# A graph network on one core: a one-column product after each group of four tiles, in the first and the fourth layer

## The chip, the cores and the metric

The kernel runs on one core of a Trainium2 chip. The metric is the device time of one execution in microseconds (us); lower is better. The engines are named as the profile names them: PE is TensorE (PEld its weight loads), DVE VectorE, ACT ScalarE, POOL GpSimd, SP SyncE. L535 is line 535 of the kernel before.

## The reference

There are 12500 nodes with 32 features and 400000 edges, sorted by their target node. Four layers follow each other; each takes h = relu(layernorm(x)) and adds its result to x. Cut to what matters:

```python
def layer0(h, edge_feat, eps, src, dst):          # 32 features on each edge
    m = relu(h[src] + edge_feat)
    return (1 + eps) * h + segment_sum(m, dst)

def layer1(h, src, dst, edge_vec, emb, norm, W1, W2): ...   # tensor product with spherical harmonics
def layer2(h, row, col):                          # degree of each node as a source
    deg = segment_sum(ones, row)
    n = rsqrt(1 + deg)
    return n * (segment_sum((n * h)[col], row) + n * h)

def layer3(h, src, dst, sh, scalars, fc_w1, fc_w2):
    hid = relu(scalars @ (fc_w1 / sqrt(8))) * sqrt(2)        # [E, 256]
    w = (hid @ (fc_w2 / sqrt(256))).reshape(E, 4, 8, 8)
    s1, v1 = h[src][:, :8], h[src][:, 8:].reshape(E, 8, 3)
    s2, v2 = sh[:, 0], sh[:, 1:4]
    out_s = A_S * (einsum('eu,euw->ew', s1 * s2, w[:, 0]) + einsum('eui,ei,euw->ew', v1, v2, w[:, 1]) / sqrt(3))
    out_v = A_V * (einsum('eu,euw,ei->ewi', s1, w[:, 2], v2) + einsum('eui,euw->ewi', v1 * s2, w[:, 3])) / sqrt(3)
    return segment_sum(concat(out_s, out_v), dst) / sqrt(E / N)
```

## The kernel before

The 400000 edges are 3125 tiles of 128 edges, one edge to a partition. Sixteen tiles (`CT`) make a chunk, four tiles (`G`) a group; there are 196 chunks. Edges of a chunk have neighbouring targets, so that their sums fall into a window of nodes. The loops are unrolled, and a scheduler fixes the order of the instructions on each engine from the program's order and its dependencies; pools of rotating buffers (`bufs`) decide how far one engine may run ahead of another.

**Layer 0** (`layer0`, L626 to L702, run by `edges`, L574). For each group POOL gathers the source rows of four tiles by one indirect DMA each (`gather`, L535). `main` adds the edge features on DVE (L663) and takes relu on ACT (L664). `tail` calls `collect` (L451): DVE makes a one-hot matrix of the targets' places in the window (`oh`, L457), and four f32 products on PE (L460) add the tiles into `ps_win`. At the end of the chunk ACT copies the window out (`wsum`, L463) and `put_late` stores it. The second half of `tail` counts how often each node is a source: DVE splits the index into `hi` and `lo` (L680 to L683), makes two bf16 one-hots `ohi` and `olo` (L687), and four bf16 products (L690) add them into the histogram `ps_deg`, which DVE adds to `deg` once a chunk (L693). The one-hots come from a pool with two buffers, `ps_win` and `ps_deg` have two buffers in PSUM each.

**Layers 1 and 2** run together (`edges12`, L760 to L1121). The change doesn't touch them.

**Layer 3** (`edges3`, L1252 to L1392). One chunk is worked on while the next one's weights are made and the one after that is gathered:

- `gather`: 16 indirect DMAs on POOL (L1274), one a tile, into one of four buffers `hs`, two chunks ahead.
- `hidden`: four times a chunk, two bf16 products (L1285) into `ps_h`, which has one buffer of two PSUM banks, and a relu on ACT into `hid` (L1287).
- `scalars`: four small operations on DVE (L1293 to L1299).
- `product(c, g)`: for each group, eight f32 products (L1310) of `hid` with the second weight make `ps_w` (two buffers of two banks). An f32 product shows as two PE records, so a group shows as 16. DVE multiplies `ps_w` with the gathered rows into `pa` (L1314), `ps` (L1316) and `pv` (L1318). `ps` is the last reader of the buffer `hs`.
- `outputs`: DVE reduces these (L1326 to L1334); `thirds` splits the result into three bf16 parts (ACT L472, DVE L474 and L476).
- `places`: ACT makes the one-hot matrix (L1340, L1341).
- `collect`: 16 bf16 products (L1346) into `ps_sum`, copied by ACT (L1349); `add`: one f32 product, the fold (L1352), and ACT's copy (L1354), which `put_late` stores.

Layer 3 uses seven PSUM banks: two for `ps_h`, four for `ps_w`, one for `ps_sum`. Its order of work for one chunk is written out by hand:

```python
for s in range(4):
    if now:
        product(now, s)
        places(now, 4 * s, 4 * s + 4)
    if c:
        ...   # s = 0: outputs, thirds; 1: thirds; 2: thirds, collect; 3: add
    if c + 1 < NW:
        hidden(cs[c + 1], s % 2, s // 2)
```

Of the kernel before, what the change touches and what calls it, by code (L numbers as in the profile page):

```python
# [8 lines left out]
F32 = mybir.dt.float32  # L9
# [5 lines left out]
PSUM = bass.MemoryType.PSUM  # L15

P = 128
D = 32
NP = 125
G = 4  # L20
# [17 lines left out]
def tiles_of(E):  # L38

    C = Q4 * B  # L40
    return E // C * (C // P) - (-(E % C) // P)
# [15 lines left out]
class GNN:  # L57
# [14 lines left out]
    def __init__(self, tc, ctx, a, out, E):  # L72
        self.tc, self.nc, self.ctx, self.a, self.out, self.E = tc, tc.nc, ctx, a, out, E
        self.N = a["x"].shape[0]
        self.J = self.N // NP
        self.T = a["src"].shape[1]
        self.CT = G * CG
        self.IT = self.CT * CPI0
        assert self.N % NP == 0 and self.T % self.IT == 0
        dram = ctx.enter_context(tc.tile_pool(name="dram", bufs=1, space=bass.MemoryType.DRAM))  # L80
        rows = self.N + P
        self.tabs = [
            [dram.tile([rows, D], F32, name=f"acc{l}_{k}", tag=f"acc{l}_{k}") for k in range(NTAB)]
            for l in range(4)
        ]
        self.feats = [dram.tile([rows, D], F32, name=f"feat{l}", tag=f"feat{l}") for l in range(4)]
        self.NW = self.T // self.CT
        self.real = tiles_of(E)


        self.emb8 = dram.tile([9, 8, self.NW, Q4 * B], BF16, name="emb8", tag="emb8")
        self.emb10 = dram.tile([9, 10, self.NW, Q4 * B], BF16, name="emb10", tag="emb10")
        self.mid = dram.tile([rows, D + 1], F32, name="mid", tag="mid")
        self.local = dram.tile([P, self.NW, self.CT + 1], F32, name="local", tag="local")
        self.n_e = dram.tile([P, self.T, 3], F32, name="n_e", tag="n_e")
        self.loc_t = dram.tile([self.NW, Q4 * B], F32, name="loc_t", tag="loc_t")
        self.n_t = dram.tile([4, self.NW, Q4 * B], F32, name="n_t", tag="n_t")
        self.dst_rows = dram.tile([P, self.T], I32, name="dst_rows", tag="dst_rows")
# [367 lines left out]
    def thirds(self, pool, c, step):  # L466
# [8 lines left out]
        else:  # L475
            nc.vector.tensor_tensor(c["f3"][:, :, 2, :], c["f"], c["f3"][:, :, 1, :], op=ALU.subtract)  # L476

    def get(self, pool, l, c):

        c["win"] = pool.tile([P, D], F32, name="win")  # L480
        self.nc.sync.dma_start(c["win"], self.feats[l][ds(self.first(c), P), :])
# [144 lines left out]
    def layer0(self):  # L626
        nc, tc, J = self.nc, self.tc, self.J
        if not self.fast:
            with tc.tile_pool(name="rest", bufs=1) as pool:
                for _ in self.rest(pool):  # L630
                    pass
        with ExitStack() as ctx:
            rest = None
            if self.fast:
                self.resident(ctx)
                rest = self.rest(ctx.enter_context(tc.tile_pool(name="rest", bufs=1)))
                for _ in range(TABS[0]):
                    next(rest)
            big = ctx.enter_context(tc.tile_pool(name="big0", bufs=LEAD + 4 if self.fast else 2))
            gp = ctx.enter_context(tc.tile_pool(name="gather0", bufs=AHEAD + 2))  # L640
            wp = ctx.enter_context(tc.tile_pool(name="work0", bufs=2))
            psum = ctx.enter_context(tc.tile_pool(name="psum0", bufs=2, space=PSUM))
            hist = ctx.enter_context(tc.tile_pool(name="hist0", bufs=2, space=PSUM))

            def load(col):
                if self.fast:
                    c = {"edge_attr_32": self.load(big, "edge_attr_32", col)}
                else:
                    c = {n: self.load(big, n, col) for n in ("src", "dst", "edge_attr_32")}
                    c["row"] = self.load_row(big, "dst_t", col)  # L650
                    c["rows"] = big.tile([P, self.CT], I32, name="rows")
                c["col"] = col
                return c

            def gather(c, t0):
                return self.gather(gp, "hs", 0, c["src"], t0, c)

            def front(c, t0, hs):
                return None

            def main(c, t0, hs, _):
                m = wp.tile([P, G, D], F32, name="m", bufs=3)
                nc.vector.tensor_add(m, hs, c["edge_attr_32"][:, t0 : t0 + G, :])  # L663
                nc.scalar.activation(m, m, AF.Relu)  # L664
                return m

            def tail(c, t0, m):
                if self.fast:
                    self.collect(0, wp, psum, c, m, t0)
                else:  # L670
                    eq = self.same(wp, c["dst"], c["row"], t0)
                    self.firsts(wp, eq, c["dst"], c["rows"], t0)
                    self.scatter(0, wp, psum, eq, m, c["rows"], t0)

                if t0 == 0:
                    c["deg"] = hist.tile([P, P], F32, name="ps_deg")
                hi = wp.tile([P, G], F32, name="hi")
                lo = wp.tile([P, G], F32, name="lo")
                s = c["src"][:, t0 : t0 + G]
                nc.vector.tensor_scalar(hi, s, -0.5 * (J - 1), 1.0 / J, op0=ALU.add, op1=ALU.mult)  # L680
                nc.vector.tensor_scalar_add(hi, hi, ROUND)
                nc.vector.tensor_scalar_add(hi, hi, -ROUND)
                nc.vector.scalar_tensor_tensor(lo, hi, -float(J), s, op0=ALU.mult, op1=ALU.add)  # L683
                ohi = wp.tile([P, G, NP], BF16, name="ohi")
                olo = wp.tile([P, G, J], BF16, name="olo")
                for oh, v, n in ((ohi, hi, NP), (olo, lo, J)):
                    nc.vector.tensor_tensor(oh, self.iota[:, None, :n].to_broadcast([P, G, n]),  # L687
                                            v[:, :, None].to_broadcast([P, G, n]), op=ALU.is_equal)
                for k in range(G):
                    nc.tensor.matmul(c["deg"][:NP, :J], lhsT=ohi[:, k, :], rhs=olo[:, k, :],  # L690
                                     start=t0 + k == 0, stop=t0 + k == self.CT - 1)
                if t0 + G == self.CT:
                    nc.vector.tensor_add(self.deg, self.deg, c["deg"][:NP, :J])  # L693
                    if not self.fast:
                        nc.scalar.dma_start(self.dst_rows[:, ds(c["col"], self.CT)], c["rows"])

            self.edges(load, gather, front, main, tail,
                       windowed=(lambda c, row: c.update(self.places_of(big, row), src=self.sources_of(c))) if self.fast else None, beside=rest)
        with tc.tile_pool(name="end0", bufs=1) as pool:
            agg = self.gather_sum(0, pool)  # L700
            nc.vector.tensor_add(self.x, self.x, agg)
            nc.vector.scalar_tensor_tensor(self.x, self.h, self.eps1, self.x, op0=ALU.mult, op1=ALU.add)  # L702
# [549 lines left out]
    def edges3(self):  # L1252

        nc, tc, CT = self.nc, self.tc, self.CT
        with ExitStack() as ctx:
# [3 lines left out]
            ph = ctx.enter_context(tc.tile_pool(name="ph3", bufs=1, space=PSUM))  # L1259
            pw = ctx.enter_context(tc.tile_pool(name="pw3", bufs=2, space=PSUM))  # L1260
            ps = ctx.enter_context(tc.tile_pool(name="ps3", bufs=1, space=PSUM))

            def fetch(c):
                row = c["no"]
# [25 lines left out]
            def scalars(c):  # L1290
# [7 lines left out]
                vv = c["vv"] = wp.tile([P, CT, 3, 8], F32, name="vv")  # L1298
                nc.vector.tensor_mul(vv.rearrange("p g i u -> p g (i u)"), hs[:, :, 8:32], sh[:, :, 0:1].to_broadcast([P, CT, 24]))  # L1299

            def product(c, g):

                if g == 0:
# [4 lines left out]
                for k in range(4):  # L1308
                    for m in range(2):
                        nc.tensor.matmul(w[:, k, :], lhsT=c["hid"][:, m, 4 * g + k].rearrange("p q s -> p (q s)"), rhs=self.w2b[:, m, :],  # L1310
                                         start=m == 0, stop=m == 1)
                gs = slice(4 * g, 4 * g + 4)
                hs = c["hs"][:, gs, :]
                nc.vector.tensor_mul(c["pa"][:, gs], w[:, :, 0:128].rearrange("p g (w u) -> p g w u", u=16),  # L1314
# [3 lines left out]
                nc.vector.tensor_mul(c["pv"][:, gs].rearrange("p g i (w u) -> p (g i) w u", u=8),  # L1318
                                     w[:, :, None, 192:256].to_broadcast([P, 4, 3, 64]),
                                     c["vv"][:, gs].rearrange("p g i u -> p (g i) u")[:, :, None, :].to_broadcast([P, 12, 8, 8]))  # L1320

            def outputs(c):
                sh = c["sh"]
# [225 lines left out]
```

## Time and profile before

| | |
|---|---|
| time, median of three runs | 20938.48 us (20915.86 to 20953.58) |
| the profiled execution | 20931.77 us, span 20930.0 us |
| busy: PE, DVE, POOL, ACT | 12599.4, 12740.1, 14745.9, 6408.9 us |
| layer 0, about 200 to 4700 us: PE, DVE, POOL busy in 300 to 4600 | 1709.25, 1919.45, 3127.78 of 4300 us |
| layers 1 and 2: the same in 5500 to 15400 | 6492.84, 6717.33, 7962.22 of 9900 us |
| layer 3: the same in 15500 to 20840 | 3833.59, 3470.09, 2948.99 of 5340 us |
| mean granted PE clock of the span | 0.84 |

The page has the busy time of each engine, then the span in 40 equal slices (each digit the busy share in tenths), then the chain of work that ended last, then the costliest groups. A group's line reads: line, engine, operation, output and input tile, count, then busy time and the mean ns of one, then the engine's idle time ahead of them and what ended it. The waits name the engine and line that waited, what it waited for, and the total, the number and the longest in us. A line of the timeline has the start, the length, the instruction and its count, and in brackets the idle time ahead of it. The ends of PE's products are modelled; "remote" is a wait whose releaser the trace doesn't show.

### The profile page before, as it was taken

How to read it: one execution, taken by the hardware profiler on the slowest of the kernel's cores; microseconds unless marked ns; L12 is line 12 of the kernel's file. 1: busy time of each engine (PE TensorE's matmuls, PEld its weight loads, DVE VectorE, ACT ScalarE, POOL GpSimd, SP SyncE). 2: the span in 40 equal slices, each digit the busy share in tenths (PEclk: the TensorE clock that was granted, in tenths of full speed). 3: DMA queues.
4: the chain of work that ended last, by engine and by line, in shares of the span. 5: the costliest groups of instructions: out<-in, count | busy, mean ns of one | idle time of the engine just before them, and what ended most of it. 6: DMA issues, size and time to landing. Idle time of an engine off the chain costs nothing.

```text
span 20930.0 us, 189759 instructions
## 1 busy us (share of the span) xinstructions
PE 12599.4 (60%) x56444; PEld 6767.2 (32%) x56444; DVE 12740.1 (61%) x25505; ACT 6408.9 (31%) x13844; POOL 14745.9 (70%) x12508
## 2 busy tenths in 40 slices
PE   2443433334766666666666666666637777777776
PEld 2333433331211111111111111111125555555554
DVE  3554444334766666666666666666746666666666
ACT  0001110002333333333333333333324444444444
POOL 5777777774788888888888888888755555555553
PEclk9999999998777777777777777777768888888888
DMA  2113332112444444444444444444411111111111
GB/s 96 46 45 111 113 91 74 23 23 72 98 89 90 88 91 90 89 89 90 90 90 90 90 90 90 90 90 90 92 39 23 23 23 23 23 23 23 23 23 30
DMA packets 1482594, 1406.96 MB, mean 67 GB/s; under 512 B 1055751, under 2 KB 1250897, under 8 KB 1426409
## 3 DMA queue, kind: packets, MB, share of 16 engines
q1 hardware_dynamic: 668550, 1143.45, 17.2%
q0 software_dynamic: 750000, 205.60, 12.0%
q10 hardware_dynamic: 62992, 45.63, 0.7%
q8 instruction: 448, 7.34, 0.1%
q14 instruction: 604, 4.94, 0.1%
HBM read 1156.82 MB, written 236.20 MB: 67 GB/s over the span
## 4 chain that ended last, share of the span: by engine, by line
DVE 27%; issue 20%; PE 15%; POOL 14%; another core or an unknown queue 13%; ACT 7%; DMA 4%; DVEq 0%; ACTq 0%; SPq 0%; POOLq 0%
DVE z L853 6%; POOL acc L1008 5%; POOL hs L809 5%; PE ps_w L1310 5%; POOL hs L535 4%; PE ps_y L850 4%; DVE pv L1318 1%; DMA hs<-feat,src_all 1%; PE ps_o L860 1%; ACT oh L1340 1%; DVE f L1327 1%; DVE pa L1314 1%; ACT X L834 1%; PE ps_sum L1346 1%
## 5 line engine op out<-in xcount | busy, mean ns | idle before, releaser
L1008 POOL DMA_INDIRECT acc<-summed,rows x3125 | 5141.5, 1645 | 999.8 <-issue 882.0
L1274 POOL DMA_INDIRECT hs<-feat,src_all x3125 | 3017.6, 966 | 2462.6 <-DVE ps L1316 1460.3
L535 POOL DMA_INDIRECT hs<-feat,src_all x3125 | 3375.3, 1080 | 1368.4 <-issue 864.4
L809 POOL DMA_INDIRECT hs<-feat,src x3125 | 3210.6, 1027 | 1190.2 <-issue 944.4
L1310 PE MATMUL ps_w<-w2b,hid 128*128 128x256 f32 x12544 | 3194.7, 411 | 68.8 <-issue 53.4
L853 DVE TENSOR_TENSOR z<-ps_y,hid 128x1024 f32<-128x1024 f32 x2352 | 2837.7, 1214 | 411.2 <-PE ps_y L850 161.2
L850 PE MATMUL ps_y<-X,w2t 64*128 64x512 f32 x4704 | 2380.0, 744 | 1132.0 <-DVE z L853 656.2
L1310 PEld LDWEIGHTS ps_w<-w2b,hid 128*128 128x128 f32 x12544 | 2577.7, 209 | 625.8 <-issue 85.8
L850 PE MATMUL ps_y<-Q,w2t 64*128 64x512 f32 x4704 | 1677.6, 838 | 1678.1 <-DVE z L853 1163.8
L460 PE MATMUL ps_win<-m,oh 128*128 128x32 f32 x6272 | 1472.7, 400 | 854.9 <-ACT m L664 211.4
L472 ACT CAST f<-f 128x512 bf16<-128x512 f32 x784 | 481.2, 614 | 4785.3 <-DVE f L878 3878.6
L860 PE MATMUL ps_o<-z,sums 128*32 128x512 f32 x9408 | 1746.1, 700 | 30.0 <-DVE r L865 21.4
L460 PEld LDWEIGHTS ps_win<-m,oh 128*128 128x128 f32 x6272 | 1396.3, 328 | 927.7 <-issue 528.3
L690 PE MATMUL ps_deg<-olo,ohi 128*125 128x100 bf16 x3136 | 462.8, 298 | 2001.6 <-DVE olo L687 1416.9
L1287 ACT ACTIVATE hid<-ps_h 128x1024 f32<-128x1024 f32 x784 | 802.0, 1023 | 2368.0 <-remote 1923.5
L1314 DVE TENSOR_TENSOR pa<-ps_w,q 128x512 f32<-128x512 f32 x784 | 540.1, 689 | 1605.5 <-remote 1407.0
L824 DVE STREAM_TRANSPOSE X<-hs 128x512 f32<-128x512 f32 x392 | 273.4, 700 | 1999.8 <-DMA hs<-feat,src 1328.8
L850 PEld LDWEIGHTS ps_y<-Q,w2t 64*128 64x128 f32 x4704 | 521.2, 256 | 2923.8 <-DVE z L853 1578.9
L850 PEld LDWEIGHTS ps_y<-X,w2t 64*128 64x128 f32 x4704 | 614.2, 210 | 2343.2 <-DVE z L853 1159.5
L663 DVE TENSOR_TENSOR m<-hs,edge_attr 128x128 f32<-128x128 f32 x784 | 228.3, 291 | 1609.6 <-issue 779.8
L664 ACT ACTIVATE m<-m 128x128 f32<-128x128 f32 x784 | 240.3, 310 | 3145.1 <-DVE m L663 1175.9
L690 PEld LDWEIGHTS <-ohi 128*125 128x125 bf16 x3136 | 445.7, 215 | 1990.8 <-DVE ohi L687 1035.7
(207 smaller groups left out, 19667.1 us busy)
## 6 DMA issues: line engine op xcount, KB each, us to landing
has<-loc_t SPq DMA_DIRECT2D x392, 1024.0 KB
srow<-in_src_t SPq DMA_DIRECT2D x392, 512.0 KB
N<-n_t SPq DMA_DIRECT2D x3136, 32.0 KB
hs<-feat,src_all POOLq DMA_INDIRECT x6250
emb<-pp SPq DMA_DIRECT2D x252, 280.0 KB
emb<-emb SPq DMA_DIRECT2D x196, 360.0 KB
emb<-pp SPq DMA_DIRECT2D x252, 224.0 KB
emb<-emb SPq DMA_DIRECT2D x196, 288.0 KB
```

The costliest lines, as they stand in the source:

```text
L460: nc.tensor.matmul(c["sum"], lhsT=oh[:, k, :], rhs=feat[:, k, :], start=t0 + k == 0, stop=t0 + k == self.CT - 1)
L535: self.nc.gpsimd.indirect_dma_start(out=t[:, k, :], out_offset=None, in_=self.feats[l][:], in_offset=bass.IndirectOffsetOnAxis(ap=idx[:, t ...
L690: nc.tensor.matmul(c["deg"][:NP, :J], lhsT=ohi[:, k, :], rhs=olo[:, k, :], start=t0 + k == 0, stop=t0 + k == self.CT - 1)
L809: nc.gpsimd.indirect_dma_start(out=c["hs"][:, k, :], out_offset=None, in_=self.feats[1][:], in_offset=bass.IndirectOffsetOnAxis(ap=c["src" ...
L850: nc.tensor.matmul(y[:, q, :], lhsT=self.w2t[64 * q : 64 * q + 64, h, j, :], rhs=c["Q" if j < 3 else "X"][64 * q : 64 * q + 64, h, :], sta ...
L853: nc.vector.tensor_mul(z, y, c["hid"][:, 2 * h : 2 * h + 2, :])
L860: nc.tensor.matmul(c["o", j // 3][32 * q : 32 * q + 32, :], lhsT=self.sums[:, j, :], rhs=c["z", j, q % 2][:, q // 2, :], start=j % 3 == 0, ...
L1008: nc.gpsimd.indirect_dma_start(out=self.tabs[2][k % NTAB][:], out_offset=bass.IndirectOffsetOnAxis(ap=c["rows"][:, G * g + k : G * g + k + ...
L1274: nc.gpsimd.indirect_dma_start(out=c["hs"][:, k, :], out_offset=None, in_=self.feats[3][:], in_offset=bass.IndirectOffsetOnAxis(ap=c["src" ...
L1287: nc.scalar.activation(c["hid"][:, m, :, 2 * h : 2 * h + 2, :].rearrange("p b q s -> p q b s"), t.rearrange("p q (b s) -> p q b s", s=32), ...
L1310: nc.tensor.matmul(w[:, k, :], lhsT=c["hid"][:, m, 4 * g + k].rearrange("p q s -> p (q s)"), rhs=self.w2b[:, m, :], start=m == 0, stop=m == 1)
L1314: nc.vector.tensor_mul(c["pa"][:, gs], w[:, :, 0:128].rearrange("p g (w u) -> p g w u", u=16), c["q"][:, gs, None, :].to_broadcast([P, 4, ...
```

## The change

A method `settle` makes one product with 32 rows of output and a single column, into the tile `ps_t`. The pools for it, `after0` and `after3`, lie in PSUM and have one buffer, so each such product waits for the one before it. Nothing reads `ps_t`. In layer 0 it follows the four histogram products of a group and takes its operands from the last of the group's one-hots. In layer 3 it follows the eight products of a group and takes its operands from the `pv` that DVE wrote for the group before; there is none after the very first group. Layer 3 then uses all eight PSUM banks. The scheduler places each product in PE's stream: in layer 0 right behind its group's L690, in layer 3 ahead of the L1310 group that comes next (once a chunk behind the first of that group's products, and once behind L1346).

```diff
+    def settle(self, pool, lhsT, rhs):
+
+        for _ in range(self.settles):                 # self.settles = 1
+            t = pool.tile([D, 1], F32, name="ps_t")
+            self.nc.tensor.matmul(t, lhsT=lhsT, rhs=rhs, start=True, stop=True)
...
+            after = ctx.enter_context(tc.tile_pool(name="after0", bufs=1, space=PSUM))
...
                 for k in range(G):
                     nc.tensor.matmul(c["deg"][:NP, :J], lhsT=ohi[:, k, :], rhs=olo[:, k, :],
                                      start=t0 + k == 0, stop=t0 + k == self.CT - 1)
+                if self.fast:
+                    self.settle(after, ohi[:, G - 1, :D], olo[:, G - 1, 0:1])
...
+            after = ctx.enter_context(tc.tile_pool(name="after3", bufs=1, space=PSUM))
...
+            state = []
+
             def product(c, g):
...
                     for m in range(2):
                         nc.tensor.matmul(w[:, k, :], lhsT=c["hid"][:, m, 4 * g + k].rearrange("p q s -> p (q s)"), rhs=self.w2b[:, m, :],
                                          start=m == 0, stop=m == 1)
+                if state:
+                    self.settle(after, *state)
...
+                state[:] = c["pv"][:, 4 * g, 0, 0:D], c["pv"][:, 4 * g, 1, 0:1]
```

More of the change, by code (lines that the diff above doesn't have):

```diff
@@ L87, in __init__ @@
         self.NW = self.T // self.CT
+        self.settles = 1
         self.real = tiles_of(E)
```

## The prediction

> **What bounds the kernel now.** I read the page first: the slices show three stages, and the change touches the first (slices 1 to 9, layer 0) and the last (slices 31 to 40, layer 3).
>
> ```profile
> PE   2443433334766666666666666666637777777776
> POOL 5777777774788888888888888888755555555553
> PEclk9999999998777777777777777777768888888888
> DVE 27%; issue 20%; PE 15%; POOL 14%; another core or an unknown queue 13%; ACT 7%; DMA 4%; DVEq 0%; ACTq 0%; SPq 0%; POOLq 0%
> ```
>
> No engine is full in either. One core runs, so "another core or an unknown queue" means waits whose releaser the trace lacks. Next the groups and the waits of layer 0 (200 to 4600 us; first line) and of layer 3 (15500 to 20840 us):
>
> ```profile
> L535 POOL DMA_INDIRECT hs<-feat,src_all x2953 | 3197.3, 1083 | 1204.1 <-issue 817.4 <-DVE lo L683 190.7 <-DVE hi L681 68.1
> L1274 POOL DMA_INDIRECT hs<-feat,src_all x3053 | 2949.1, 966 | 2319.2 <-DVE ps L1316 1446.9 <-issue 872.4
> ACT hid L1287 <- remote: 1855.8, 305, 12.2
> POOL hs L1274 <- DVE ps L1316: 1446.9, 191, 11.8
> DVE pa L1314 <- remote: 1362.3, 235, 12.3
> ```
>
> Layer 0 is POOL's: 3197 us of gathers and 817 us between them fill 4015 of 4400. In layer 3 POOL waits for DVE once a chunk, and DVE and ACT wait for "remote". What that is, the timeline of one chunk shows (17043 to 17063):
>
> ```profile
> 17044.77 3.72 PE L1310 MATMUL ps_w<-w2b,hid 128*128 128x256 f32 x16 [0.54 <-issue]
> 17048.33 0.60 PE L1285 MATMUL ps_h<-emb,w1s 72*128 72x512 bf16 x2
> 17048.76 3.62 PE L1310 MATMUL ps_w<-w2b,hid 128*128 128x256 f32 x16
> 17055.44 0.95 POOL L1274 DMA_INDIRECT hs<-feat,src_all  x1 [0.30 <-issue]
> 17058.78 0.69 DVE L1314 TENSOR_TENSOR pa<-ps_w,q 128x512 f32<-128x512 f32 x1 [9.47 <-remote]
> 17058.82 1.02 ACT L1287 ACTIVATE hid<-ps_h 128x1024 f32<-128x1024 f32 x1 [10.24 <-remote]
> ```
>
> The third product of the chunk (call the four W0 to W3) ends at 17048.49 and the hidden product at 17048.93, yet both readers start at 17058.8, 2.4 us after POOL's last gather. PE's completion signals come late during a train of gathers. In layer 3 every signal due in the first two microseconds of a train is on time, one due at 8 to 10 us almost never, and one due after 12 us is held to the train's end plus 2.4 to 3 us. The chunk's cycle is this: train 20.2 us (16 gathers of 0.966 and 0.30 between), release at 22.9, DVE's W2 and W3 until 26.9, next train at 27.2. A chunk is 27.2 us, 196 of them 5340 us. PE is needed at one point only: W3 must have ended by about 25.9, when DVE takes it.
>
> **The change, part by part.** Durations are of the profiled execution: 20931.8 us, span 20930.0, 6.7 us under the median of 20938.5. Its measurement can tell about 0.2% (42 us) from no change.
>
> *Layer 0.* 784 bf16 products, each with a 32-column load, right after a group's four histogram products (L690). Nearest row: four L690 products in a stretch of 0.56 us, 0.14 each, so 110 us of PE in a stage where PE is 40% busy and POOL sets the end: nothing on the path. Without that cover they cost 110. Each waits for the one before (one buffer), and 107 writes of `ohi` (L687) now wait for PE. If a signal is held, PE stops one group earlier than before; behind it are L460 and L690 of the next group, and POOL runs on by its prefetch. The two largest "remote" groups of this stage, ACT L463 and DVE L693, count 44 and 34 waits, up to 39 us; one more round of 1.9 + 0.56 us (an L460 and an L690 group) at each of the 78 would be 190 us. Bounds 0 to +190, unless a signal is hastened (rival A); I take +15, near the lower end, because POOL is 91% occupied.
>
> *Layer 3.* 783 f32 products. The build moves each ahead of the next L1310 group: one right behind L1346 (collect), one inside W0 after its first product, one ahead of W2, one ahead of W3. Each takes over the wait for DVE's `pv` (L1318) that the first product of that group has now, so no new wait for DVE arises. New are the waits for the settling product before it: W0's for collect's, collect's for the previous chunk's, W3's for W2's. Queued behind are the L1310 group and the L1285 of the next hidden product; ACT `hid` (L1287) and DVE `pa` (L1314) wait for those. Price of one: the fold L1352 (96x32, f32) takes 0.41 us for its two records; a one-column product should not take more warm, and 0.82 at half clock; the lower bound is 0.1, a load row of 105 ns (L1285). I take 0.41, the nearest shape: 783 x 0.41 = 321 us of PE. On the path stands what lies ahead of a deadline. The collect's runs before W0's own wait for `pv` and is absorbed. W2's and W3's run ahead of W3, which in an undisturbed chunk ends at 16.5 and is needed at 25.9.
>
> What is left is W0's: it pushes the hidden products, and their signals fall where lateness grows. The trace holds this experiment. Chunks alternate between two kinds. In 94 early ones (27.20 us) the third of the four hidden products is issued at 7.7 us, its signal is 1.8 us late, and all of it is swallowed. In 85 late ones (mean 28.04) it is issued at 9.0 to 10.3, its signal is late by 5 to 12 us, the fourth waits for it, and W3 behind that runs 6.42 us instead of 3.62. Sorted by the issue of that third product: 9.4 to 9.8, period 27.8 (48 chunks); 9.8 to 10.3, 28.8 (27 chunks). So 0.4 us later costs +0.75 us, on half of 196 chunks: +74 us. If all late chunks went early it would be 85 x 0.84 = -71; if all were held to the train's end, 31.0 (three chunks do this now), +3.0 x 98 = +294.
>
> The clock: W3 at 6.42 against 3.62 us is PE after 3 to 9 us without work. The Trainium skill's "TensorE: Matmul & The Clock Gate", Part 1, states that an idle window of about 3.4 us halves the clock; by it a product placed into the gap would save up to 2.8 us per late chunk. Here the build puts it behind the gap, next to the group, so I count nothing. [...]
>
> ACT's order in layer 3 moves too: in each chunk the copy L1354 goes ahead of one `hid` (L1287, 1.02 us). L1354 is 0.18 us and its fold has just ended by then: nothing, or 0.2 us if late, beside ACT's 46% load.
>
> Sum: 15 + 74 = 89 us: 21,021 against 20,931.8, or 21,028 on the median.
>
> **Rivals.** *A: the small product brings the signals on time.* It would be so if a product's completion became visible only when another, waiting one follows. For: both touched stages suffer from late signals, and in layer 0 signals are on time more often where PE goes on at once. Against: in the timeline above W2's signal stayed away while two hidden products and sixteen L1310 records followed, and these 16-record groups wait for DVE as the new product will. Price: the chunk falls to its floor, the train's 20.3 or PE's 0.72 x 27.25 = 19.6 plus the settling 1.6, some 21.2: -6 x 196 = -1180, and in layer 0 up to POOL's 386 us of waits. Full: about 19,500; for layer 0 or part of the chunks alone: 20,300 to 20,850.
>
> *B: the settling product holds PE.* W3's waits for W2's, due about 9.4 us into the train in early chunks and 10 or more in late ones. If that signal is held to the release at 22.9, W3 (6.4 us cold) runs to 29.3 instead of being ready at 25.9: +3.4 us. It decides from the point at which W2's signal is more than 8 us late. Signals due at 9.3 to 9.7 were 5 to 8.7 late, so early chunks pass (W3 at 15 to 18) and late ones are on the edge. Late ones alone go to about 31: +290; all: 3.4 x 196 = +670. Time 21,200 to 21,600, likeliest 21,260. For: one-buffer waits go through the very signals that are late. Against: L1310 carries waits for PE's own signals now, and idles 67 us in all.
>
> *C: all is hidden.* The 0.41 us fall into PE's waits and late chunks stay as they are: 20,900 to 20,980. For: 9 us of slack on most chunks. Against: the two classes above differ by 1 us.
>
> **How the numbers follow.** Forecast (small loss, 20,980 to 21,180) 0.40; B 0.17; C 0.13; A 0.30, half of it full, half partial. Faster is A, 0.30; same is C, 0.13; slower is the forecast and B, 0.57. The likeliest single case is the forecast: 21,030. Its own bounds are the terms' ends, +40 to +250. The whole range must reach into A for its partial half, to 20,250, and up over B to 21,550, which leaves out the full A (0.15) and B's extreme (0.03).
>
> **What would show it.** Right: in the profile after, the train of L1274 stays at 966 ns and 0.30, "remote" of `hid` and `pa` keeps 1300 to 2000 us each, early chunks stay at 27.2, and more chunks reach 28 to 31. The settling rows read 0.1 to 0.4 us. Layer 0 ends at the same time within 50 us. B would show as L1310 or the settling line waiting for PE's own line, 100 us or more in total. A would show as the "remote" rows falling to a few hundred us and POOL no longer waiting for `ps` L1316, with POOL's share of slices 31 to 40 rising from 5 to 7. I am wrong if layer 3 is shorter than 5250 us or longer than 5500, or if layer 0 moves by over 100.

## The result, and the profile after

The changed kernel takes 21146.25 us in the median (21124.56 to 21203.92, four runs) beside 20939.74 us of the kernel before: a ratio of 1.0104, 95% interval 1.0082 to 1.0126. It is slower by 206 us; 21030 was predicted. The profiled execution took 21124.56 us (span 21122.8), 193 us more than the one before.

All of it is in layer 3. From the first to the last gather of a stage, read in the timeline, layer 0 lasts 4667.0 us (4673.2 before), the stretch between the two layers is 3 us longer, and layer 3 lasts 5568.5 us (5371.6 before). The page after, slices and chain:

```profile
PE   3444344444766666666666666666557777777776
POOL 5777777764788888888888888888745555555553
PEclk9999999998777777777777777777678888888888
DVE 25%; PE 23%; issue 17%; another core or an unknown queue 14%; POOL 11%; ACT 7%; DMA 3%; DVEq 0%; ACTq 0%; SPq 0%; POOLq 0%
```

PE is busier in layer 0 (3 and 4 for 2 to 4) with no effect on its length, and its share of the chain is up from 15% to 23%. The waits of layer 3 (15430 to 21040 us):

```profile
POOL hs L1285 <- DVE ps L1331: 1650.6, 192, 16.6
ACT hid L1298 <- remote: 1460.9, 212, 24.8
DVE pa L1329 <- remote: 1233.0, 211, 36.1
PE ps_t L483 <- remote: 337.6, 112, 36.8
```

The first of these rows in the kernel before, over all of its layer 3 (15430 to 20930 us):

```profile
POOL hs L1274 <- DVE ps L1316: 1460.3, 192, 13.5
```

POOL waits 190 us more for the end of the chunk; that is the loss. The late signals ("remote" of `hid` and `pa`) are still there, and the small product `ps_t` has a "remote" wait of its own. In layer 0 that last wait is larger, and free (70 to 4800 us):

```profile
PE ps_t L483 <- remote: 933.7, 82, 30.5
```

Of 191 chunks with a whole train, sorted by the issue of the third hidden product: before, 95 early ones at 27.18 us and 96 late ones at 28.02; after, 112 early ones at 27.33 and 79 late ones at 30.44. The mean goes from 27.60 to 28.62 us, times 196 chunks +200 us, which is the whole difference. One late chunk, whose train starts at 16893.5 us, in the timeline after:

```profile
16894.88 1.20 PE L1323 MATMUL ps_w<-w2b,hid 128*128 128x256 f32 x2
...
16896.01 0.27 PE L483 MATMUL ps_t<-pv 128*32 128x1 f32 x2
...
16896.21 5.89 PE L1323 MATMUL ps_w<-w2b,hid 128*128 128x256 f32 x16
...
16915.58 0.69 DVE L1329 TENSOR_TENSOR pa<-ps_w,q 128x512 f32<-128x512 f32 x1 [10.43 <-remote]
16916.29 1.02 ACT L1298 ACTIVATE hid<-ps_h 128x1024 f32<-128x1024 f32 x1 [10.04 <-remote]
16917.36 1.01 PE L1296 MATMUL ps_h<-emb,w1s 72*128 72x512 bf16 x2 [7.57 <-ACT hid L1298]
...
16918.72 6.57 PE L1323 MATMUL ps_w<-w2b,hid 128*128 128x256 f32 x16
```

The first product W0 starts cold (PE at half of its clock) and stays cold to its end, 8.6 us into the train. The third hidden product is issued at 11.9 and its signal held to 22.8; the fourth waits for `hid`; W3 follows cold, ends at 31.8, and the next train starts at 33.1 instead of 27.2. The granted clock goes up at 16900.64, as three stretches of this chunk show, the first from 2.1 us behind the start of the cold collect at 16891.69 (columns: length, then busy time of PE, PEld, DVE, ACT and POOL, then the clock):

```profile
16893.81:16897.23 3.42, 3.42 (x12) 2.21 (x12) 3.42 (x5) 2.84 (x9) 2.72 (x3) 0.50 0.35 95
16897.23:16900.64 3.41, 3.41 (x10) 2.69 (x9) 3.30 (x2) 2.24 (x6) 2.58 (x3) 0.50 0.13 25
16900.64:16904.05 3.41, 3.41 (x17) 2.83 (x16) 1.91 (x4) 1.48 (x3) 2.50 (x4) 1.00 0.06 10
```

In a late chunk of the kernel before, whose collect starts at 17006.85, one such stretch is enough:

```profile
17007.44:17010.85 3.41, 3.41 (x20) 2.81 (x19) 3.41 (x7) 1.73 (x5) 1.88 (x2) 0.50 0.12 16
17010.85:17014.26 3.41, 3.41 (x18) 2.90 (x17) 3.41 (x2) 3.30 (x10) 2.50 (x4) 1.00 0.37 98
```

PE is busy throughout in all five.

### The profile page after: what moved, and what is told of

It reads as the page before. It is cut to its first block, busy times and chain, and to the rows that moved or that the text cites. A ratio compares the mean times of both kernels' runs of the same rounds, so it can differ in the third digit from the quotient of the medians.

```text
span 21122.8 us, 194655 instructions
## 1 busy us (share of the span) xinstructions
PE 13099.9 (62%) x58794; PEld 7003.3 (33%) x58794; DVE 12749.4 (60%) x25505; ACT 6357.9 (30%) x13844; POOL 14726.9 (70%) x12508
## 4 chain that ended last, share of the span: by engine, by line
DVE 25%; PE 23%; issue 17%; another core or an unknown queue 14%; POOL 11%; ACT 7%; DMA 3%; DVEq 0%; ACTq 0%; SPq 0%; POOLq 0%
PE ps_w L1323 9%; DVE z L863 6%; PE ps_y L860 4%; POOL acc L1018 4%; POOL hs L819 4%; POOL hs L542 2%; PE ps_win L461 2%; PE ps_o L870 1%; PE ps_h L1296 1%; ACT X L844 1%; ACT oh L1356 1%; DVE cnt L1000 1%; DVE eq L995 1%; DVE summed L1014 1%
## 5 line engine op out<-in xcount | busy, mean ns | idle before, releaser
L1323 PE MATMUL ps_w<-w2b,hid 128*128 128x256 f32 x12544 | 3461.5, 432 | 46.6 <-issue 45.5
L1323 PEld LDWEIGHTS ps_w<-w2b,hid 128*128 128x128 f32 x12544 | 2646.9, 218 | 506.5 <-issue 42.4
L895 ACT ACTIVATE oh<-iota,local 128x128 bf16<-128x128 f32 x3136 | 1014.2, 389 | 75.6 <-DMA local<-local 75.6
```

The source lines that it names most:

```text
L895: nc.scalar.activation(c["oh"][:, k, :], self.iota, AF.Square, bias=c["local"][:, k : k + 1], scale=-1.0)
```

## The experiments

The expectations name two theories: the hold (a small product waits for another's late signal) and the push (work ahead of the hidden products moves them to where signals are held). Kernels of a group ran together on one chip, beside the kernel before.

**Which layer.** Layer 0's products alone:

```diff
-                if state:
-                    self.settle(after, *state)
```

> The small product in layer 0 alone, none in layer 3. Both theories on layer 3 (the hold and the push, see the next ones) say that layer 0 is covered by POOL's gathers: the train of layer 0 lasts 4673 us before and 4667 with the whole change. Expected: within 0.2% of the kernel before (20900 to 20980 us), layer 0 at 4650 to 4700 us, layer 3 at 5372 from the first to the last gather. If part of the 206 us is made in layer 0 and only shows later (state left behind by a delayed start of layer 3), 20990 or more.

Measured: 20925.57 us, ratio 0.9999 (0.9989 to 1.0009). Layer 0 lasts 4674.6 us, layer 3 5381.8. Layer 0's products cost nothing, though they wait 958 us for late signals in this run.

**Which of the four.** From here layer 0's call is taken out, and layer 3 keeps a part. The two ahead of the third and the fourth product:

```diff
-                if state:
+                if state and g in (1, 2):
```

> Layer 3 alone, and only the two small products that stand ahead of the third and the fourth product of a chunk; the second of them waits for the first. Theory hold: that wait keeps the fourth product back until a late signal arrives; the fourth product then ends some 4 us before the collect instead of 9, PE's clock is low in the next chunk's first product, and that chunk's hidden product signals too late. All of the loss is here: 21100 to 21180 us, layer 3 at 5540 to 5600, two kinds of chunk at 27.2 and about 31.5. Theory push (0.4 us of work ahead of the hidden products): these two stand behind the hidden products that matter, so the time is that of the kernel before, 20900 to 20980.

Measured: 21153.43 us, 1.0110 (1.0088 to 1.0132), in the hold's range and outside the push's. The two at the chunk's border:

```diff
-                if state:
+                if state and g in (0, 3):
```

> Layer 3 alone, and only the two small products at the chunk's border (behind the collect and inside the first product). Each still waits for the one before it, but those signals fall outside a train or in its first two microseconds. Theory hold: 20900 to 20990 us. Theory push: the 0.4 us stand ahead of the hidden products: by my forecast's term +74 us, by the whole loss +200, so 21000 to 21150.

Measured: 21252.44 us, 1.0157 (1.0135 to 1.0179), above the ranges of both. And all four without a wait for each other:

```diff
+            cells = after.tile([D, 8], F32, name="ps_t")
...
-                if state:
-                    self.settle(after, *state)
+                if state:
+                    u = (4 * c["no"] + g) % 8
+                    nc.tensor.matmul(cells[:, u : u + 1], lhsT=state[0], rhs=state[1], start=True, stop=True)
```

> Layer 3 alone, all four small products a chunk, but into eight columns of one PSUM tile in turn, so that none waits for another small product; their wait for DVE's pv and their work stay. Theory hold: the loss goes, 20890 to 20990 us. Theory push, or a cost of the work itself: the loss stays, 21100 to 21180. In between (21000 to 21080): both.

Measured: 21320.29 us, 1.0193 (1.0170 to 1.0216). This refutes the hold as the cause of the whole loss: without it the loss is nearly twice as large. Its waits in layer 3 show no wait of a small product among the largest, and more "remote" for `hid` and `pa`:

```profile
POOL hs L1283 <- DVE ps L1331: 1857.1, 192, 16.1
ACT hid L1296 <- remote: 1685.8, 209, 43.2
DVE pa L1329 <- remote: 1558.7, 245, 34.9
```

The parts don't add up either, each pair alone being as bad as the four together. The hold exists, as the run with the two inner products shows in its timeline:

```profile
17189.14 1.01 PE L1294 MATMUL ps_h<-emb,w1s 72*128 72x512 bf16 x2 [4.88 <-ACT hid L1296]
...
17193.04 0.27 PE L483 MATMUL ps_t<-pv 128*32 128x1 f32 x2 [2.89 <-remote]
...
17193.23 5.81 PE L1321 MATMUL ps_w<-w2b,hid 128*128 128x256 f32 x16
```

W3 could start at 17190.2 and waits for the train's end; its late chunks take 30.3 us. But in early chunks the same hold puts W3 closer to the collect, so that PE goes into the next chunk with less idle time. Chunks whose collect runs cold (over 1.7 us instead of 1.1) number 93 of 186 before, 90 in the run without the hold, and 46 in the changed kernel. So the single buffer gives back about half of what the products cost (206 against 390 us).

**One small product.** The one behind the collect, the one inside W0, and the latter with 192 columns:

```diff
+                if state and g == 3:      # behind the collect
...
+                if state and g == 0:      # inside the first product
...
+            t = pool.tile([D, 192], F32, name="ps_t")     # and rhs = c["pv"][:, 4 * g], all columns
```

> Layer 3 alone, only the small product behind the collect. The runs before refuted the hold as the whole cause: without any wait of one small product for another the loss doubled (+390 us), and in every run with a small product at the chunk's border PE reaches full clock about 8.5 us after the collect's start instead of 5.5, so that the chunk's first product ends near 9.7 and its hidden products' signals fall due after 11 us, where they are held to the train's end. Theory clock: which of the two border products delays the clock is open. If the one inside the first product does it alone, this run gives 20910 to 20970 us and the clock at 5.5; if any extra product at the border does, 21100 to 21250 and 8.5.

> Layer 3 alone, only the small product inside the chunk's first product, behind its first two records. Theory clock, with the product inside the first product as its cause: 21150 to 21300 us, full clock about 8.5 us after the collect's start in chunks that begin cold, every second chunk at 30 to 33 us. If it is the sum of the border's two products (some 0.8 us of cold work), half of that: 21030 to 21120.

> As the run before, but the product inside the first product has 192 columns instead of one: the same place and the same operand's wait, with more PE work. Theory clock in the form that a nearly empty product (one column, a load each) thins PE's activity so that the clock comes up one step later: the wide product is ordinary work, the clock comes up at 5.5 to 6 us, and the time falls to 20920 to 21020 although the work grows. Theory push (work ahead of the hidden products): 0.4 to 0.8 us more ahead of them, so at least the time of the run before, 21200 to 21350.

Measured: 21201.97 us (1.0116, 1.0099 to 1.0133), 21184.86 us (1.0106, 1.0089 to 1.0122), and 21278.13 us (1.0154, 1.0136 to 1.0172). Each alone costs as much as the whole change. I had expected one of the first two to cost little, and missed. The wide product costs more than the narrow one, as the push has it, and not less: a thin product is not what keeps the clock low.

The runs have in common that a late third hidden product goes with a long chunk. In the nine kernels so far (the one before, the changed one and seven experiments), 1719 chunks, by the issue of the third hidden product from the train's start:

| issue of the third, us | chunks | fourth issued at | period |
|---|---|---|---|
| 7 to 9 | 890 | 13.4 | 27.3 |
| 9.0 to 9.4 | 70 | 17.4 | 27.7 |
| 9.4 to 9.8 | 111 | 19.7 | 28.1 |
| 9.8 to 10.2 | 128 | 21.2 | 29.8 |
| 10.2 to 10.6 | 104 | 21.4 | 30.2 |
| 10.6 to 11 | 86 | 23.1 | 31.4 |
| 11 to 14 | 330 | 23.6 | 31.4 |

The table pools kernels, and the issue alone does not set the period. Between 9.8 and 10.6 us, 25 chunks of the kernel before last 28.8 us and 41 of the run with layer 0's products alone 28.4, but 53 of the run with the product behind the collect 30.9; the reader `hid` of the third product starts at 19.9 and 19.4 us there, and at 22.0 here. So its signal also comes later at the same issue; why is not known.

The late chunks' mean issue and period are 9.66 and 28.0 before, 10.10 and 30.3 with the two inner products (where the hold adds its part), 10.67 and 31.0 behind the collect, 10.81 and 30.0 inside W0, 10.87 and 30.4 with the change, 11.32 and 31.5 wide, 11.54 and 32.0 without the hold, 11.60 and 31.3 with the two at the border.

Why a product of 0.27 us moves the third hidden product by 1.2 us is seen in cold chunks, timed from the collect's start. Inside W0: W0 starts at 2.87 us and `hid` at 2.83 in this run and in the kernel before alike, but W0 is done at 8.97 instead of 7.76 in the mean. Behind the collect, W0 starts at 3.19 and is done at 8.78. The schedule also moved the copy L1370 (L1354 before) ahead of `hid` on ACT there, and `hid` starts at 3.49 instead of 2.83; but W0's records follow each other without a pause, so no wait for `hid` shows.

Most of the rest is the clock. In layer 3 of all these runs the granted clock is 0.5 or 1.0 and changes only on a grid of 3.413 us that runs on through the chunks (405 changes in the kernel before, all within 0.004 us of it). Take the first whole step of the grid behind the start of a cold collect. In the kernel before and in the runs with layer 0's products alone and with the two inner products, the clock is up at the end of that step in all 283 cold chunks. With the product behind the collect, which runs from 1.87 to 2.14 us, it is up in all 53 chunks whose step starts later than 2.0 us, and one step later in all 40 whose step starts earlier; W0 is done at 8.24 and 9.48 us. The step is missed in 51 of 95 cold chunks inside W0, in 52 of 92 with the wide product, in 37 of 48 with the change, in 80 of 92 with the two at the border and in 70 of 92 without the hold. What a step must hold to count is open: busy time does not decide it. Nor is the missed step the whole loss: behind the collect, the chunks that miss it last 31.1 us and the others 30.9.

**The train.** The rest tests where the late signals come from. POOL's gathers in four parts, first with a copy on POOL ahead of each:

```diff
+                if done is not None:
+                    nc.gpsimd.tensor_copy(wp.tile([P, 1], F32, name="go"), done)
-                for k in self.rows_for(c["hs"], CT, c, 0):
+                for k in c["rows"][k0:k1]:
...
+                        gather(cs[c + 2], 4 * s, 4 * s + 4, now["pa"][:, 4 * s, 0, 0:1])
```

> The kernel before with POOL paced: the 16 gathers of a chunk are issued in four parts, each behind a one-column copy on POOL that reads the pa of the current chunk's group. It tests what the whole explanation rests on, that PE's signals are late because of the long train. Theory train: with trains of four gathers (5 us) the signals come on time, 'remote' of hid and pa falls from 1856 and 1362 us to under 400 each, a chunk falls from 27.3 to 21 to 24 us, and the time to 19800 to 20400. If the lateness has nothing to do with the train's length, the copies cost 0 to 200 us: 20930 to 21150.

Measured: 21174.00 us, 1.0097 (1.0080 to 1.0114). The four copies stand together ahead of the 16 gathers, so the train is as long and this says nothing on it. (Its late chunks, without any small product, have their third product at 9.54 us and last 30.9: again more than the issue tells.) Then with the copy into the gather's own target, on the kernel before and on the changed one:

```diff
-                    nc.gpsimd.tensor_copy(wp.tile([P, 1], F32, name="go"), done)
+                    nc.gpsimd.tensor_copy(c["hs"][:, k0:k1, 0:1], done)
...
-                            gather(cs[c + 2], 4 * s, 4 * s + 4, now["pa"][:, 4 * s, 0, 0:1])
+                            gather(cs[c + 2], 4 * s, 4 * s + 4, now["pa"][:, 4 * s : 4 * s + 4, 0, 0:1])
```

> The kernel before with POOL's gathers held apart: in the run called paced the scheduler set the four copies one behind the other ahead of the train, so the train stayed 20 us long and nothing was tested. Here each part of four gathers first gets one column written by POOL from the pa of the current chunk's group, so that its gathers can't move ahead of it. Theory train: trains of 5 us, the signals on time, a chunk of 21 to 24 us in place of 27.3, 19700 to 20400 us. If the lateness has nothing to do with the train: 20930 to 21200.

> The changed kernel with the same pacing. If the whole loss of the change comes by way of late signals (small products push hidden products to where their signals are held), then without long trains the change costs only its PE work: 0 to 0.8 us a chunk against the run paced2, 0 to 160 us, and nothing at all where POOL sets the pace. If the small products cost by themselves, the difference to paced2 is 200 us or more.

Measured: 20672.01 us, 0.9862 (0.9845 to 0.9880), and 20999.57 us, 1.0035 (1.0021 to 1.0050). The first is faster than both kernels, but far from 20400, and the change costs 328 us on top of it, not 0 to 160. The groups of the first, in layer 3, say why:

```profile
L1291 ACT ACTIVATE hid<-ps_h 128x1024 f32<-128x1024 f32 x773 | 788.2, 1020 | 743.8 <-PE ps_h L1289 332.7 <-PE ps_sum L1356 110.4 <-issue 106.5
L1353 ACT COPY s<-ps_sum 96x128 f32<-96x128 f32 x192 | 50.1, 261 | 1848.4 <-remote 1770.0 <-issue 63.1 <-PE ps_h L1289 9.9
```

"Remote" of `hid` is gone from the top, but the collect's reader now has 1770 us of it. Where `pa` is ready, the parts follow each other without a pause, and 16 gathers in a row stand from 17010.7 to 17031.3 us. Of 199 stretches of gathers without a pause of over 1 us, 188 hold 16 (191 of 193 in the kernel before). The pacing moved the train against the products; it hardly shortened it. With the change on top, most trains do fall into 12 and 4 gathers (143 and 142 stretches), and the collect's reader still waits 1821.5 us for "remote". With the train moved, another signal is late; that a short train has no late signals was not tested, and the 328 us are not explained.

**ACT's order.** The last step of the loop with the hidden product ahead of `add`, for the change and for the product behind the collect alone:

```diff
-                        else:
-                            add(last)
                     if c + 1 < NW:
                         hidden(cs[c + 1], s % 2, s // 2)
+                    if c and s == 3:
+                        add(last)
```

> The changed kernel with the last step of layer 3's loop written with the hidden product ahead of add. PE's stream stays the same; on ACT the hid that the next chunk's first product needs stands ahead of the copy L1370 again, as in the kernel before (one operation of 0.4 us stays ahead of it). In cold chunks hid starts 3.5 us after the collect's start in the changed kernel and 2.8 in the one before, and the first product waits for it. Theory ACT order: a large part of the loss comes from there; 20980 to 21080 us, and the first product done at 8 to 9 us after the collect in cold chunks in place of 9.8. Theory PE work (the small products themselves): ACT's order is worth nothing, 21110 to 21180.

> Layer 3 with only the small product behind the collect (1.0116 before), with the same reversal of ACT's order. That small product is 0.27 us of PE and its kernel differs from the one before in ACT's order besides. Theory ACT order: most of the 240 us go, 20950 to 21060. Theory PE work: 21160 to 21230 as without the reversal.

Measured: 18880.42 us, 0.9976 (0.9967 to 0.9986), and 18888.25 us, 0.9981 (0.9971 to 0.9991). These can't be set beside the others: in this group the kernel before itself took 18929.45 us. The chip was another one, and on it no signal is late. Groups of layer 3 (14800 to 18700 us) of the change with ACT's order reversed:

```profile
L1285 POOL DMA_INDIRECT hs<-feat,src_all x3077 | 2962.8, 963 | 937.7 <-issue 875.9 <-DMA hs<-feat,src_all 54.9 <-DVE f L477 5.8
L1298 ACT ACTIVATE hid<-ps_h 128x1024 f32<-128x1024 f32 x767 | 778.1, 1014 | 619.9 <-PE ps_h L1296 619.9
L1329 DVE TENSOR_TENSOR pa<-ps_w,q 128x512 f32<-128x512 f32 x767 | 522.0, 681 | 15.1 <-PE ps_w L1323 14.4
```

There is no "remote" at all; POOL never waits for `ps`, and layer 3 lasts 3960.9 us, 20.2 a chunk, which is POOL's own time. The gathers take 963 ns (966 in the kernel before and 968 in the changed one on the other chips), and all 3125 follow each other without a pause of over 1 us: on this chip an unbroken train makes no signal late. So these runs leave the question of ACT's order open: the loss that it was to split doesn't exist there. Both kernels are 41 to 49 us faster than the one before, with the order and the products changed together; beside the run with one product, the other three and layer 0's cost nothing where signals are on time.

## Why the prediction was right or wrong

The time lies in the range and on the side that was forecast; the likeliest value was 116 us too low.

- *The mechanism of the forecast* held in part: small products push the third hidden product of chunks that begin cold to where its signal is held, the fourth and W3 follow late. *Its size was wrong.* The term "0.4 us later" measured 1.2 us (9.66 to 10.87), and one product takes 0.22 us, or 0.27 cold, instead of 0.41. The failing step is the one on the clock, "so I count nothing": most of the delay is not the product's length but PE's clock, which in many cold chunks comes up one step of 3.41 us later behind it. Such a step at half clock is some 1.7 us of work (an estimate); in 40 of 93 chunks that is 0.7 of the 1.0 us by which the product behind the collect moves the third product. The page that I set against the row, "TensorE: Matmul & The Clock Gate" of the Trainium skill, Part 1, has the clock rise after a busy window of about 3.4 us. The length of the step agrees with the trace; the rest does not, since PE was busy 3.42 us of such a step in the late chunk above and the clock stayed at 0.50 for one more, and the measurement decides.
- *The price for a chunk* was read too low as well: 0.75 us for 0.4, from bins that ended at 10.3 us (75 chunks). W3 takes 5.4 us in the mean of the late chunks before, not the 6.42 of the one that was read. In the pooled table the steep part lies between 9.4 and 11, but part of that is a difference between kernels: at the same issue the changed ones run some 2 us longer, and nothing here tells why.
- *ACT's order*, "nothing, or 0.2 us": `hid` starts 0.66 us later in cold chunks. No wait of W0 for it shows; what the order is worth by itself is open.
- *The collect's product*, "absorbed": alone with its move on ACT it costs 1.16%. Wrong.
- *Layer 0*, 15 us: right, 0.9999 alone.
- *Rival B*: its wait is there (338 us in layer 3), and with the inner pair alone it lengthens late chunks to 30.3, a loss of 223 us, near the 290 that I gave for late chunks alone. In the whole change it works the other way, since it halves the number of cold chunks. There its price had the wrong sign. That the loss is no further from the forecast's 89 us owes something to luck, since the hold, left out of the forecast, takes off part of it: without the hold the small products cost 390 us.
- *Rival A*: refuted in its claim; `hid` and `pa` keep 1461 and 1233 us of "remote". Its floor for a chunk was nearly right, though not by its reason: without late signals a chunk is 20.2 us (I had 21.2), and the kernel before is 2000 us faster on the chip that has none (I had 1180 for layer 3 and up to 386 for layer 0).
- *Rival C*: refuted by the late chunks, 28.0 to 30.4.
- I had named layer 3 over 5500 us as a sign of being wrong; it was 5568, from the sizes above.

## What to carry to other kernels

In a stage that runs as a cycle with a deadline, price an added instruction by what it does to the time of the one signal that has a deadline, and read a first price from the spread that the kernel already shows between its own repetitions; here that price was too low, so only a run settled it. A wait and the work it guards can have opposite signs: taking the wait away here nearly doubled the loss. Sort the repetitions of a loop before averaging: here 1% was two chunks in five getting 2.4 us longer, and no group of the page shows that.

## What the runs showed of the hardware

- PE's completion signals are late while POOL issues a long train of gathers, by up to 10 us, and the last come some 2.4 us after the train. This holds on the chips of the first three groups (the kernel before at 20930 to 20964 us) and not on that of the fourth (18929), where in the profile of the change with ACT's order reversed all 2693 signals of PE looked at in layer 3 (14800 to 18700 us) came with the products' ends. The train is longer there, all of layer 3 without a pause. The cause was not found. Beside the profile of the changed kernel, layer 0 (4191 us instead of 4667) and layer 3 (3961 instead of 5568) carry 2083 of 2248 us.
- PE's granted clock changes only on a grid of 3.413 us. In cold chunks, most of them after 7 to 9 us without work, it rises 4.0 to 6.5 us after the collect's start in the kernel before (95 chunks), always at the end of the first whole step of the grid. With small products at the chunk's border it rises in the median 6.4 (one behind the collect) to 8.8 us after it (the change), because steps are missed. What makes a step count is open: a product of 0.27 us in it can spoil it, and a wider one doesn't help.
- A version faster than both kernels came of the pacing, 0.9862 (0.9845 to 0.9880), by setting the train against other products.
